# A four-layer convolution network on one core: statistics as a pipeline of loads, group norms split in pieces, earlier pacing of layer 1, and longer runs in layer 2

## The chip, the cores and the metric

The kernel runs on one core of one Trainium2 chip. The metric is the device time of one execution in microseconds (us), and the comparison is made with the median of several executions. Fewer microseconds is better. The core's engines are named as in the profile: PE multiplies matrices (PEld is its load of weights), DVE works on vectors, ACT evaluates functions and copies, POOL is a general vector engine, and SP issues most transfers. Transfers of all queues run on 16 DMA engines.

## The reference

The input x has shape (4, 384, 64, 64). There are four layers, each of the form x = x + layer(gn(x)), where gn is a group norm over 32 groups of 12 channels, without weights:

```python
def _gn(v, G=32, eps=1e-5):
    g = v.reshape(B_, G, C_ // G, H_, W_)
    m = jnp.mean(g, axis=(2, 3, 4), keepdims=True)
    s = jnp.var(g, axis=(2, 3, 4), keepdims=True)
    return ((g - m) / jnp.sqrt(s + eps)).reshape(v.shape)

# layer 0: attention of 4096 positions on the first 96 channels
q, k, v = split(bn(w_qkv @ layer_norm(x[:, :96])))
out = v @ softmax(q^T k / 4)^T
y = bn(w_proj @ relu(concat(out, x[:, 96:])))
# layer 1: w_in, a filter on 8x8 patches by FFT, a 3x3 depthwise convolution
t = dwconv3(irfft2(rfft2(patches(w_in @ x)) * fft_filter))
y = w_out @ (gelu(t[:192]) * t[192:])
# layer 2: depthwise 3x3 and 5x5, each with a norm over batch and image
tok = bn(kw0 * bn(dw3(x)) + kw1 * bn(dw5(x)) + x * c1_w + c1_b)
tok = tok * sigmoid(...);  ch = tok + bn(cm_w2 @ gelu(bn(cm_w1 @ tok)))
y = gate * ch + (1 - gate) * x
# layer 3: a depthwise 7x7 convolution whose kernel is made from mean and maximum of x
```

## The kernel before

**Layers 0 and 1 (phase_a).** The 384 channels lie as three column groups (j = 0, 1, 2) of 128 partitions; an image is 4096 columns, taken in 8 tiles of 512. `attention(b)` works one batch of layer 0 in 64 steps: 8 query tiles by 8 blocks of keys, each step some score matmuls, an exponential on ACT and the `av` matmuls. Beside it `side_by_side` advances a second generator, `others(b)`: the statistics of x for the next batch (`x_norm(b + 1)`), layer 1 of the batch before (`layer1(b - 1)`), and the queries, keys and values of the next batch (`qkv(b + 1)`). Every piece yields its weight, and `per_step` says how much weight is to be done by which attention step. Layer 1 of the last batch runs after the attention, alone. A framework places the instructions on the engines in an order that it works out from the program; within an engine they run in that order.

`x_norm(b)` loads 24 tiles of 128 x 512 (two buffers "xs", for batch 0 nine buffers that the queries take later), and has DVE run bn_stats on each right after its load. `norm_of_stats` aggregates them and `norm_of_groups` turns them into the group norm: a sum over channels on PE (`gn_pg`), a subtraction and squares on DVE, again PE (`gn_pv`), and a reciprocal square root. For batch 0 all this stands ahead of everything else, and `centered`, the first step of `qkv`, then loads the first 96 channels again (`ln_x`). Between the two stands a branch on a bound for the scores; its other side isn't taken here. `layer0_end` leaves statistics from which `norm1` is made when the attention of a batch ends; `layer1` begins with it.

**Layer 2's convolutions (phase_b).** A unit is 32 channels of all four batches; there are 12 units, and each has 16 calls of `conv53`, for two channels each. One call multiplies the image strips `z` with banded Toeplitz matrices (`toep`) that hold both kernel sizes, 3x3 and 5x5; 12 matmuls come from it. `matrices53(n)` builds a matrix by multiplying taps (`w53`, 320 KB for four calls, loaded by `taps53`) with a band mask, on DVE for even n and the first four, on POOL for the rest; it runs two calls ahead, with four buffers. `conv53` copies the result from PSUM into `d_o` (ACT), takes its statistics (bn_stats on DVE), and after every fourth call writes d_o to the scratch tensors `d53`, one for each kernel size, in runs of 4 KB. `conv_norms(u)` ends the unit: it makes scale and shift of both sizes from the statistics (`cn_rep` and `cn_m` on PE, in between ACT and DVE). During the next unit `unit_tok(u)` reads d53 back (`c_d`, 96 reads of 512 KB in all, whose runs are 512 bytes), adds the two sizes and the input (`tok_m`), and stores the sum to `tok`. `unit_strips(u + 1)` loads the next unit's input (`unit_x`, 2048 columns), normalizes it on ACT and transposes it on PE (`strip_m`) into z. Strips and tok take turns, one piece behind each conv53. The loads, the reads of d53 and the stores of tok are issued on SP's queue, the writes of d53 on ACT's.

After the last unit, `tok_stats` waits for the last sums, and the 1x1 convolutions of layer 2 (phase_ef) and layer 3 (phase_g) follow; the change does not touch these.

Of the kernel before, what the change touches and what calls it, by code (L numbers as in the profile page):

```python
# [40 lines left out]
UNITS = C // 32  # L41

# [238 lines left out]
class _Builder:  # L281
    def __init__(self, ctx, tc, ins, out):
# [32 lines left out]
        self.d53 = [  # L315
            [self.dram.tile([32, B, 32, P], F32, tag=f"d{i}{u}", name=f"d_{i}_{u}") for u in range(UNITS)]
            for i in range(2)
        ]
# [110 lines left out]
    def norm_of_groups(self, mv):  # L429
# [7 lines left out]
        nc.vector.tensor_add(d[:, :, 0], d[:, :, 0], mv[:, :, 1])  # L437
        pv = self.of_groups("gn_pv", d)[:, :, 0]
# [69 lines left out]
    def phase_a(self, strips):  # L508
# [3 lines left out]
        with ExitStack() as ctx:  # L512
# [8 lines left out]
            self.probs = attention.enter_context(tc.tile_pool(name="a_probs", bufs=2, side="right"))  # L521
            self.center = self.const(cp, "center", PD)
# [8 lines left out]
            for k in ("r0", "m0", "n0"):  # L531
                setattr(self, k, cp.tile([P, NJ, B], F32, tag=k, name=k))
            self.qkv_weights(cp)
            for _ in self.x_norm(0):
                pass
# [6 lines left out]
            for _ in self.qkv(0, q, k4, vt):  # L542
                pass
# [38 lines left out]
    def others(self, b, nxt):  # L582

        if b + 1 < B:
            yield from self.x_norm(b + 1)
# [7 lines left out]
    def side_by_side(self, b, steps, others):  # L595

        per_step = ((176 if b else 0) + (42 if b + 1 < B else 0)) / 64
# [20 lines left out]
    def norm_of_stats(self, st):  # L618
        mv = self.sm([P, NJ, 2], "gn_mv")
        for j in range(NJ):  # L620
            self.nc.vector.bn_aggr(mv[:, j, :], st[:, j].rearrange("p a b -> p (a b)"))
        return self.norm_of_groups(mv)
# [8 lines left out]
    def x_norm(self, b):  # L631

        st = self.stats_tile("x_st")
        for i in range(8):
            for j in range(NJ):

                x = self.wk("x_in", "xs", 2) if b else self.big.tile([P, 512], F32, tag="q", name="x_in0", bufs=9)
                self.nc.sync.dma_start(x, self.ins["x"][b][:, j, i * 512 : (i + 1) * 512])
                self.nc.vector.bn_stats(st[:, j, i, :], x)
            yield 0.5  # L640
        r, gm, n, _ = self.norm_of_stats(st)
# [3 lines left out]
    def centered(self, b, i):  # L645
# [4 lines left out]
        nc.sync.dma_start(x, self.ins["x"][b][0:PD, 0, i * 512 : (i + 1) * 512])  # L650
        nc.vector.tensor_scalar(
            x, x, self.m0[0:PD, 0, b : b + 1], self.r0[0:PD, 0, b : b + 1], ALU.subtract, ALU.mult
# [27 lines left out]
    def qkv(self, b, q, k4, vt):  # L680
# [3 lines left out]
        xc[0] = self.centered(b, 0)  # L684
        yield 1.0
        xn[0] = self.layer_norm(xc[0])
        xc[1] = self.centered(b, 1)
        yield 2.0
        for i in range(8):
            if i + 2 < 8:  # L690
                xc[i + 2] = self.centered(b, i + 2)
# [1343 lines left out]
```

## Time and profile before

| what | value |
|---|---|
| median of 3 executions | 4879.94 us (4866.37 to 4882.83) |
| the profiled execution, its own time | 4868.55 us |
| span of the profiled execution, first to last instruction | 4866.7 us |
| PE's mean granted clock, full speed being 1 | 0.950 |
| DMA packets in all | 345857, of which 172295 under 2 KB |
| first exponential of the attention | at 75.2 us |
| layers 0 and 1 beside each other end, layer 1 of batch 3 starts | 2161 to 2201 us |
| layer 2: convolutions | 2478 to 3045 us |
| layer 2: first 1x1 convolution | at 3087.8 us |
| layer 3 | 4096 to 4867 us |

The times in the lower rows are counted from the span's first instruction. The profile covers one execution, so its durations add up to that execution's time and not to the median. PE is counted as busy while a matmul is in flight, at whatever clock it was granted: a stretch with a clock of 0.5 can be full and still slow. The costliest groups of instructions in layer 2's convolutions have these lines (line, engine, operation, output and inputs, shapes, count; busy time and mean of one in ns; idle time of the engine before them with what ended most of it):

```profile
L1289 POOL TENSOR_TENSOR toep<-w,band 128x1280 f32<-128x1280 f32 x94 | 272.2, 2900 | 307.0 <-PE conv_m L1308 201.1
L1308 PE MATMUL conv_m<-toep,z 128*128 128x192 f32 (+1 forms) x2304 | 447.0, 356 | 17.8 <-DVE toep L1289 17.6
```

An idle engine costs nothing by itself: POOL is idle for 307.0 us there since its matrices are needed no sooner than PE's convolutions free their buffers.

### The profile page before, as it was taken

The page shows a single profiled execution, that of the slowest core. Times are in us where ns is not written, and L with a number is a line of the kernel's source. Part 1 is how long each engine was busy: PE and PEld are TensorE (multiplying, and loading weights), DVE is VectorE, ACT ScalarE, POOL GpSimd, SP SyncE. Part 2 cuts the span into 40 slices and gives each one's busy share as a digit, 9 for nine tenths or more (in the row PEclk, how much of TensorE's full clock was granted, in tenths as well). Part 3 has the DMA queues.
Part 4 walks back from the last instruction along what each step waited for, and adds up shares of the span by engine and source line. Part 5 has one row for each costly group of instructions (what it writes and reads, how often), then busy time and mean ns, then how long its engine had stood idle before and what let it go on. Part 6 is the DMA issues. An engine that isn't in the chain of part 4 may idle for free. (4 is left out here: it accounts for less than half of the span.)

```text
span 4866.7 us, 49663 instructions
## 1 busy us (share of the span) xinstructions
PE 4413.5 (91%) x18441; PEld 2456.1 (50%) x18441; DVE 2901.2 (60%) x4642; ACT 1998.2 (41%) x2974; POOL 728.9 (15%) x594
## 2 busy tenths in 40 slices
PE   6899999999999999988978889699999997778888
PEld 2233444344443444435468888344444443667888
DVE  6766566655566455566867778555521113667898
ACT  3454344444444443436345556211133334753321
POOL 1000000000000000000034445000000001225544
PEclk8999999999999999999989989899999998788999
DMA  4211212121211111113259999866664444895776
GB/s 159 79 51 48 80 65 72 46 79 33 75 55 67 48 52 52 64 51 124 73 176 296 280 286 308 279 254 253 239 236 151 156 156 160 314 341 185 230 255 232
DMA packets 345857, 749.23 MB, mean 154 GB/s; under 512 B 22684, under 2 KB 172295, under 8 KB 336647
## 3 DMA queue, kind: packets, MB, share of 16 engines
q1 hardware_dynamic: 279864, 471.92, 31.3%
q0 software_dynamic: 32640, 151.28, 7.9%
q10 hardware_dynamic: 33102, 122.77, 6.5%
q8 instruction: 149, 2.44, 0.2%
q14 instruction: 102, 0.83, 0.1%
HBM read 443.62 MB, written 302.25 MB: 153 GB/s over the span
## 5 line engine op out<-in xcount | busy, mean ns | idle before, releaser
L788 ACT ACTIVATE probs<-sc_s 128x1024 f32<-128x1024 f32 x512 | 496.8, 1020 | 690.6 <-PE av L898 588.2
L898 PE MATMUL av<-probs,vt 128*128 128x512 f32 x1536 | 714.9, 602 | 0.0
L1097 DVE SCALAR_TENSOR_TENSOR acc<-band,vecs,acc 128x512 f32<-128x512 f32 x708 | 496.4, 746 | 45.2 <-POOL band L1058 40.0
L1591 PE MATMUL h_m<-f_h,cm_w_t 128*128 128x512 f32 x1152 | 497.4, 595 | 7.4 <-ACT f_h L1579 7.4
L1308 PE MATMUL conv_m<-toep,z 128*128 128x192 f32 (+1 forms) x2304 | 447.0, 356 | 17.8 <-DVE toep L1289 17.6
L898 PEld LDWEIGHTS av<-probs,vt 128*128 128x128 f32 x1536 | 275.6, 191 | 338.1 <-issue 334.4
L1308 PEld LDWEIGHTS conv_m<-toep,z 128*128 128x128 f32 x2304 | 410.9, 198 | 41.0 <-issue 10.1
L1905 PE MATMUL conv_m<-toep,z 128*128 128x128 f32 x3072 | 393.6, 286 | 37.9 <-POOL toep L1892 19.6
L1905 PEld LDWEIGHTS conv_m<-toep,z 128*128 128x128 f32 x3072 | 379.3, 202 | 39.9 <-POOL toep L1892 19.9
L1537 PE MATMUL h_s<-e_tok,cm_w_t 128*128 128x512 f32 x768 | 363.3, 596 | 4.2 <-DVE e_tok L1522 4.2
L1591 PEld LDWEIGHTS h_m<-f_h,cm_w_t 128*128 128x128 f32 x1152 | 219.8, 191 | 285.0 <-issue 273.9
L780 PE MATMUL sc_s<-q,k 32*128 32x512 f32 x2048 | 310.7, 644 | 19.4 <-ACT probs L788 19.1
L1599 DVE BATCH_NORM_STATS2 h_st<-f_h 128x6 f32<-128x512 f32 x96 | 66.4, 693 | 429.9 <-ACT f_h L1598 429.9
L1289 POOL TENSOR_TENSOR toep<-w,band 128x1280 f32<-128x1280 f32 x94 | 272.2, 2900 | 307.0 <-PE conv_m L1308 201.1
L1020 PE MATMUL t_m<-w_in_t,xb 128*128 128x384 f32 x768 | 279.7, 499 | 4.3 <-DVE coef L1037 4.1
L934 PE MATMUL proj_m<-xm,w_proj_t 128*128 128x512 f32 x576 | 271.6, 611 | 4.9 <-DVE xm L873 4.9
L1544 ACT COPY e_h<-h_s 128x1024 f32<-128x1024 f32 x96 | 97.2, 1012 | 400.3 <-PE h_s L1537 400.3
L1546 DVE BATCH_NORM_STATS2 h_st<-e_h 128x6 f32<-128x512 f32 x192 | 123.5, 685 | 203.8 <-ACT e_h L1544 203.8
L1537 PEld LDWEIGHTS h_s<-e_tok,cm_w_t 128*128 128x128 f32 x768 | 146.6, 191 | 188.7 <-issue 183.3
L941 DVE SCALAR_TENSOR_TENSOR x_res<-proj_m,bn_c,x_res 128x512 f32<-128x512 f32 x96 | 71.8, 748 | 241.0 <-PE proj_m L934 240.8
L1020 PEld LDWEIGHTS t_m<-w_in_t,xb 128*128 128x128 f32 x768 | 143.3, 193 | 142.0 <-issue 60.7
L1537 PE MATMUL h_s<-z,cm_w_t 128*128 128x512 f32 x384 | 196.1, 592 | 0.0
(408 smaller groups left out, 6383.4 us busy)
## 6 DMA issues: line engine op xcount, KB each, us to landing
d<-d_o ACTq DMA_DIRECT2D x96, 512.0 KB
c_d<-d SPq DMA_DIRECT2D x96, 512.0 KB
hid<-e_h ACTq DMA_DIRECT2D x16, 3072.0 KB
f_h<-hid SPq DMA_DIRECT2D x16, 3072.0 KB
x_in<-in_x SPq DMA_DIRECT2D x96, 256.0 KB
x_res<-in_x SPq DMA_DIRECT2D x32, 768.0 KB
xa<-x_res POOLq DMA_DIRECT2D x32, 768.0 KB, 3.7
xa_out<-xa SPq DMA_DIRECT2D x32, 768.0 KB
```

What stands on the lines that cost most here:

```text
L780: nc.tensor.matmul(s[:, g], lhsT=k4[32 * g : 32 * g + 32, c], rhs=q[i][32 * g : 32 * g + 32], start=True, stop=True,)
L788: nc.scalar.activation(p[:, h * 1024 : (h + 1) * 1024], s[:, 2 * h : 2 * h + 2].rearrange("p a b -> p (a b)"), AF.Exp, scale=0.25,)
L898: nc.tensor.matmul(av[0], lhsT=vt[:, 4 * c + v, :], rhs=p[:, v * 512 : (v + 1) * 512], start=c == 0 and v == 0, stop=c == 7 and v == 3,)
L934: nc.tensor.matmul(m, lhsT=self.w_proj[:, j, o * P : (o + 1) * P], rhs=xm[:, j], start=j == 0, stop=j == NJ - 1,)
L1020: nc.tensor.matmul(m[:, 0:C], lhsT=xb[:, j], rhs=self.w_in[:, j, :], start=j == 0, stop=j == NJ - 1,)
L1097: nc.vector.scalar_tensor_tensor(out, src(j, k), w, done, ALU.mult, ALU.add)
L1289: eng.tensor_tensor(t, self.w53[:, at : at + 160].rearrange("p (m n) -> p m n", n=8).unsqueeze(2).to_broadcast([P, 20, 8, 8]), band.rearra ...
L1308: nc.tensor.matmul(m[:, c * 256 + to : c * 256 + to + 64 * (k1 - k0)], lhsT=self.z_[:, at : at + P], rhs=t[:, 10 * c + k0 : 10 * c + k1].r ...
L1537: nc.tensor.matmul(s[:, v, :], lhsT=w1[:, j, o * P : (o + 1) * P], rhs=t[j][:, v * 512 : (v + 1) * 512], start=j == 0, stop=j == NJ - 1,)
L1546: nc.vector.bn_stats(st[:, o, 8 * b + 2 * i + v, :], h[:, o, v * 512 : (v + 1) * 512])
L1591: nc.tensor.matmul(m, lhsT=w2[:, o, j * P : (j + 1) * P], rhs=h[:, o, v * 512 : (v + 1) * 512], start=o == 0, stop=o == 5,)
L1905: nc.tensor.matmul(m[:, ch * P : (ch + 1) * P], lhsT=self.z_[:, at : at + P], rhs=t[:, 8 * c + 2 * i : 8 * c + 2 * i + 2].rearrange("p m a ...
```

## The change

**Statistics of x.** `first_tiles` loads the eight tiles of batch 0 that hold channels 0 to 127 and keeps them; `first_norm` makes mean and scale of channels 0 to 95 from them alone, and `qkv(0)` works on the kept tiles in place of loading them again. The other 16 tiles of batch 0 are done by `x_norm(0, ...)` within `others(0)`, ahead of `x_norm(1)`. `x_norm` now asks for two tiles and takes the statistics of the two asked for a piece earlier; a piece has weight 1.2.

**Group norms.** `norm_of_groups` becomes the generator `norm_steps`, which yields between its halves; the moments are made by `moments`. At the end of a batch's attention only the moments are made (`mv1`), and `layer1` does the rest when it starts.

**Pacing.** `per_step` has other weights, and for the last batch it is divided by 57 in place of 64, so that layer 1 of batch 2 is through seven steps before the attention of batch 3 is.

**Layer 2.** One scratch tensor for a unit holds both kernel sizes side by side, so that d_o is written in runs of 8 KB (one transfer, not two) and read back in runs of 1 KB (48 reads, not 96). The sum of `unit_tok` is written over the unit's input in unit_x and stored from there. Strips are asked for two units ahead, in loads of 1024 columns, and normalized half a tile before they are transposed. `conv_norms` of a unit is issued behind the next unit's first conv53. The matrices run three calls ahead (`LEAD`) with five buffers, the taps have three buffers, and their loads are issued on POOL's queue.

```diff
-        self.d53 = [
-            [self.dram.tile([32, B, 32, P], F32, tag=f"d{i}{u}", name=f"d_{i}_{u}") for u in range(UNITS)]
-            for i in range(2)
-        ]
+        self.d53 = [self.dram.tile([32, B, 32, 2, P], F32, tag=f"d{u}", name=f"d_{u}") for u in range(UNITS)]
...
-    def norm_of_groups(self, mv):
+    def norm_steps(self, mv):
...
+        yield 0.3
...
+            for k in ("r0", "m0", "n0"):
+                setattr(self, k, cp.tile([P, NJ, B], F32, tag=k, name=k))
+            self.x0_st = self.stats_tile("x1_st")
+            self.x0 = self.first_tiles(self.x0_st)
...
             self.qkv_weights(cp)
-            for _ in self.x_norm(0):
-                pass
+            self.first_norm(self.x0_st)
...
-            for _ in self.qkv(0, q, k4, vt):
+            for _ in self.qkv(0, q, k4, vt, self.x0):
...
+        if b == 0:
+            yield from self.x_norm(0, self.x0_st, 0.5)
...
-        per_step = ((176 if b else 0) + (42 if b + 1 < B else 0)) / 64
+        per_step = ((177 if b else 5) + (55 if b + 1 < B else 0)) / (64 if b + 1 < B else 57)
...
-    def norm_of_stats(self, st):
-        mv = self.sm([P, NJ, 2], "gn_mv")
+    def moments(self, st, name="gn_mv", bufs=2):
+        mv = self.sm([P, NJ, 2], name, bufs)
         for j in range(NJ):
             self.nc.vector.bn_aggr(mv[:, j, :], st[:, j].rearrange("p a b -> p (a b)"))
-        return self.norm_of_groups(mv)
+        return mv
...
+    def first_tiles(self, st):
+        tiles = []
         for i in range(8):
-            for j in range(NJ):
-                x = self.wk("x_in", "xs", 2) if b else self.big.tile([P, 512], F32, tag="q", name="x_in0", bufs=9)
+            x = self.big.tile([P, 512], F32, tag="q", name="x_in0", bufs=9)
+            self.nc.sync.dma_start(x, self.ins["x"][0][:, 0, i * 512 : (i + 1) * 512])
+            tiles.append(x)
+        for i, x in enumerate(tiles):
+            self.nc.vector.bn_stats(st[:, 0, i, :], x)
+        return tiles
+    def first_norm(self, st):
+        nc = self.nc
+        mv = self.sm([P, 2], "gf_mv")
+        nc.vector.bn_aggr(mv, st[:, 0].rearrange("p a b -> p (a b)"))
+        m = self.pm("gf_m")
+        nc.tensor.matmul(m[:, 0:1], lhsT=self.group, rhs=mv[:, 0:1], start=True, stop=True)
+        mean = self.m0[0:PD, 0, 0:1]
+        nc.vector.tensor_copy(mean, m[0:PD, 0:1])
+        d = self.sm([P, 1], "gf_d")
+        nc.gpsimd.memset(d, 0.0)
+        nc.vector.tensor_sub(d[0:PD], mv[0:PD, 0:1], mean)
+        nc.vector.tensor_mul(d, d, d)
+        nc.vector.tensor_add(d, d, mv[:, 1:2])
+        nc.tensor.matmul(m[:, 1:2], lhsT=self.group, rhs=d, start=True, stop=True)
+        self.rsqrt(self.r0[0:PD, 0, 0:1], m[0:PD, 1:2])
+    def x_norm(self, b, known=None, piece=1.2):
+        st = self.stats_tile("x_st") if known is None else known
+        tiles = [(i, j) for i in range(8) for j in range(0 if known is None else 1, NJ)]
+        coming = []
+        for n in range(0, len(tiles) + 2, 2):
+            there, coming = coming, []
+            for i, j, x in there:
+                self.nc.vector.bn_stats(st[:, j, i, :], x)
+            for i, j in tiles[n : n + 2]:
+                x = self.wk("x_in", "xs", 2)
                 self.nc.sync.dma_start(x, self.ins["x"][b][:, j, i * 512 : (i + 1) * 512])
-                self.nc.vector.bn_stats(st[:, j, i, :], x)
-            yield 0.5
-        r, gm, n, _ = self.norm_of_stats(st)
+                coming.append((i, j, x))
+            yield piece
+        mv = self.moments(st)
+        yield 0.3
+        r, gm, n, _ = yield from self.norm_steps(mv)
...
-    def centered(self, b, i):
+    def centered(self, b, i, src=None):
         nc = self.nc
         x = self.wk("ln_x", "lx", 2)[0:PD]
-        nc.sync.dma_start(x, self.ins["x"][b][0:PD, 0, i * 512 : (i + 1) * 512])
+        if src is None:
+            src = x
+            nc.sync.dma_start(x, self.ins["x"][b][0:PD, 0, i * 512 : (i + 1) * 512])
         nc.vector.tensor_scalar(
-            x, x, self.m0[0:PD, 0, b : b + 1], self.r0[0:PD, 0, b : b + 1], ALU.subtract, ALU.mult
+            x, src[0:PD], self.m0[0:PD, 0, b : b + 1], self.r0[0:PD, 0, b : b + 1], ALU.subtract, ALU.mult
         )
         s = self.pm("ln_s")
         nc.tensor.matmul(s[0:PD], lhsT=self.center, rhs=x, start=True, stop=True)
...
-        self.norm1 = self.norm_of_stats(st)
+        self.mv1 = self.moments(st, "gn_mv1", 1)
...
-        norm, alone = self.norm1, b == B - 1
+        norm, alone = (yield from self.norm_steps(self.mv1)), b == B - 1
...
-            for n in range(4):
+            for n in range(LEAD + 2):
                 self.matrices53(n)
             for q in range(4):
...
+            strips, behind = self.unit_strips(1), None
+            next(strips)
             for u in range(UNITS):
                 st = self.bt_p.tile([P, 2, 16, 6], F32, tag="st", name="st")
-                strips = self.unit_strips(u + 1) if u + 1 < UNITS else iter(())
                 tok = self.unit_tok(u - 1) if u else self.unit_strips(0)
                 nets = iter(()) if u else self.nets(cp)
                 for n in range(16):
                     if u or n > 1:
-                        self.matrices53(16 * u + n + 2)
+                        self.matrices53(16 * u + n + LEAD)
                     self.conv53(u, n, st)
-                    next(strips if n % 2 else tok, None)
+                    if n == 0 and u:
+                        self.conv_norms(u - 1, behind)
+                    if n % 2:
+                        next(strips, None)
+                    elif n or not u:
+                        next(tok, None)
+                    if n == 15 and u:
+                        next(tok, None)
+                    if n == 14 and not u:
+                        for _ in tok:
+                            pass
                     if n % 3 == 2:
                         next(nets, None)
-                self.conv_norms(u, st)
+                    if n == 15 and u + 2 < UNITS:
+                        strips = self.unit_strips(u + 2)
+                        next(strips)
+                behind = st
+            self.conv_norms(UNITS - 1, behind)
...
-        for i in range(2):
+        tiles = self.unit_x[u]
+        def load(i):
             x = self.bx_p.tile([P, 2048], F32, tag="x", name="unit_x")
-            for b in range(B):
-                nc.sync.dma_start(
-                    x[32 * b : 32 * b + 32], self.x1[b][32 * q : 32 * q + 32, j, i * 2048 : (i + 1) * 2048]
-                )
-            self.unit_x[u].append(x)
-            for h in range(4):
-                if h % 2 == 0:
-                    xh = x[:, 512 * h : 512 * h + 1024]
-                    nc.scalar.activation(
-                        xh, xh, AF.Identity, bias=self.norm_u[:, 1, u : u + 1], scale=self.norm_u[:, 0, u : u + 1]
+            for k in range(2):
+                at = i * 2048 + k * 1024
+                for b in range(B):
+                    nc.sync.dma_start(
+                        x[32 * b : 32 * b + 32, k * 1024 : k * 1024 + 1024],
+                        self.x1[b][32 * q : 32 * q + 32, j, at : at + 1024],
                     )
...
+            tiles.append(x)
+        def norm(k):
+            x = tiles[k // 2][:, k % 2 * 1024 : k % 2 * 1024 + 1024]
+            nc.scalar.activation(
+                x, x, AF.Identity, bias=self.norm_u[:, 1, u : u + 1], scale=self.norm_u[:, 0, u : u + 1]
+            )
+        load(0)
+        norm(0)
+        yield
+        for n in range(8):
+            i, h = n // 4, n % 4
+            x = tiles[i]
+            if j:
...
+            if n == 0:
+                load(1)
+            if n % 2 and n < 7:
+                norm(n // 2 + 1)
+            yield
...
-            self.w53_ahead = self.bt_p.tile([P, 8 * 80], F32, tag="w53", name="w53")
+            self.w53_ahead = self.bt_p.tile([P, 8 * 80], F32, tag="w53", name="w53", bufs=3)
             src = self.ins["c53_t"][n // 64][:, n % 64 * 2 : n % 64 * 2 + 8]
-            self.nc.sync.dma_start(self.w53_ahead, src.rearrange("p c m n -> p (c m n)"))
+            self.nc.gpsimd.dma_start(self.w53_ahead, src.rearrange("p c m n -> p (c m n)"))
...
-        t = self.bt_p.tile([P, 20, 8, 8], F32, tag="toep", name="toep53", bufs=4)
+        t = self.bt_p.tile([P, 20, 8, 8], F32, tag="toep", name="toep53", bufs=LEAD + 2)
...
-            self.d_o = self.bt_p.tile([P, 2, 8, P], F32, tag="d_o", name="d_o")
+            self.d_o = self.bt_p.tile([P, 8, 2, P], F32, tag="d_o", name="d_o")
...
-            for v in range(2):
-                nc.scalar.dma_start(
-                    self.d53[v][u][:, :, 2 * n - 6 : 2 * n + 2].rearrange("y b c n -> (y b) (c n)"),
-                    self.d_o[:, v].rearrange("p c n -> p (c n)"),
-                )
+            nc.scalar.dma_start(
+                self.d53[u][:, :, 2 * n - 6 : 2 * n + 2].rearrange("y b c v n -> (y b) (c v n)"),
+                self.d_o.rearrange("p c v n -> p (c v n)"),
+            )
...
-            d5, d3 = (self.bc_p.tile([P, 1024], F32, tag=k, name=f"c_{k}") for k in ("d5", "d3"))
-            for v, d in enumerate((d5, d3)):
-                nc.sync.dma_start(
-                    d.rearrange("p (y n) -> p y n", n=P),
-                    self.d53[v][u][8 * i : 8 * i + 8].rearrange("y b c n -> (b c) y n"),
-                )
+            d = self.bc_p.tile([P, 8, 2, P], F32, tag="d", name="c_d")
+            o = self.unit_x[u][i // 2][:, i % 2 * 1024 : i % 2 * 1024 + 1024]
+            nc.sync.dma_start(
+                d.rearrange("p y v n -> p y (v n)"),
+                self.d53[u][8 * i : 8 * i + 8].rearrange("y b c v n -> (b c) y (v n)"),
+            )
             for h in range(2):
                 part = slice(h * 512, (h + 1) * 512)
                 last = u == UNITS - 1
                 m = self.psum.tile([P, 512], F32, tag="c" if last else "t", name="tok_m", bufs=4 if last else 1)
                 nc.scalar.activation(
-                    m, self.unit_x[u][i // 2][:, i % 2 * 1024 + h * 512 :][:, 0:512], AF.Identity, bias=s0, scale=self.vec("c1_w")[:, u : u + 1]
+                    m, o[:, part], AF.Identity, bias=s0, scale=self.vec("c1_w")[:, u : u + 1]
                 )
-                nc.vector.scalar_tensor_tensor(m, d3[:, part], s[:, 1:2], m, ALU.mult, ALU.add)
+                mv, ov = (t.rearrange("p (y n) -> p y n", n=P) for t in (m, o[:, part]))
+                of = lambda v: d[:, 4 * h : 4 * h + 4, v]
+                nc.vector.scalar_tensor_tensor(mv, of(1), s[:, 1:2], mv, ALU.mult, ALU.add)
                 k = 2 * i + h
                 nc.vector.scalar_tensor_tensor(
-                    d5[:, part], d5[:, part], s[:, 0:1], m, ALU.mult, ALU.add, accum_out=self.total[:, u, k : k + 1]
+                    ov, of(0), s[:, 0:1], mv, ALU.mult, ALU.add, accum_out=self.total[:, u, k : k + 1]
                 )
                 if h == 0:
                     yield
...
-            nc.sync.dma_start(self.tok[u, :, :, sl].rearrange("b c n -> (b c) n"), d5)
+            nc.sync.dma_start(self.tok[u, :, :, sl].rearrange("b c n -> (b c) n"), o)
```

## The prediction, made before the changed kernel ran

> **What bounds the kernel now.** I read the engine table and the slices first, then tables of busy time by stretch (stretch in us from the span's start; its length; then PE, PEld, DVE, ACT and POOL busy with instruction counts; granted clock; DMA share; GB/s), then PE's waits in the stretches where PE is short.
>
> ```profile
> PE 4413.5 (91%) x18441; PEld 2456.1 (50%) x18441; DVE 2901.2 (60%) x4642; ACT 1998.2 (41%) x2974; POOL 728.9 (15%) x594
> ...
> PE   6899999999999999988978889699999997778888
> ...
> PEclk8999999999999999999989989899999998788999
> ...
> 0.00:40.00 40.00, 3.06 (x15) 1.79 (x15) 21.02 (x65) 6.20 (x13) 11.81 (x39) 1.00 0.77 265
> 69.00:99.00 30.00, 30.00 (x59) 11.99 (x59) 15.48 (x28) 12.85 (x19) 1.56 (x3) 0.50 0.30 90
> 2140.00:2165.00 25.00, 18.61 (x41) 6.69 (x39) 23.92 (x33) 10.05 (x11) 2.04 (x5) 0.98 0.26 90
> 2165.00:2210.00 45.00, 32.39 (x59) 13.54 (x60) 20.37 (x52) 11.54 (x26) 1.45 (x2) 0.67 0.28 97
> 2478.00:2700.00 222.00, 195.83 (x1029) 181.89 (x1029) 165.25 (x342) 126.61 (x272) 109.75 (x38) 0.93 0.88 263
> 2700.00:2900.00 200.00, 175.88 (x956) 162.98 (x955) 149.33 (x299) 118.76 (x254) 92.93 (x33) 0.92 0.94 284
> 2900.00:3045.00 145.00, 129.78 (x708) 119.74 (x706) 114.22 (x232) 88.21 (x193) 69.50 (x24) 0.94 0.96 302
> 3045.00:3090.00 45.00, 6.21 (x21) 4.49 (x22) 22.23 (x77) 18.93 (x32) 0.00 (x0) 0.50 0.94 280
> ```
>
> PE is the bound of most of the span. Only where it is short can the change pay: the first 40 us, the end of batch 3's attention (2140 to 2210), layer 2's convolutions (2478 to 3045) and their drain (3045 to 3090). In the convolutions PE is busy 88% and DMA 88 to 96%. PE's waits there (2478 to 3050), as microseconds in total, times, longest:
>
> ```profile
> PE strip_m L1236 <- ACT unit_x L1229: 24.7, 10, 3.0
> PE conv_m L1308 <- DVE toep L1289: 17.6, 7, 4.9
> PE cn_m L1350 <- DVE z L1241: 6.2, 5, 3.8
> PE cn_rep L1341 <- DVE st L1322: 5.9, 4, 1.9
> PE strip_m L1236 <- ACT z L1243: 5.4, 8, 0.9
> PE cn_rep L1341 <- DVE z L1241: 3.5, 3, 1.2
> ```
>
> They are chains through one tile, not a full engine: DVE and ACT have room.
>
> **What the Trainium skill says.** "TensorE: Matmul & The Clock Gate", What's actually happening: the array runs at half rate by default and activity releases it within some 3.4 us. The 0.50 beside the idle drain agrees; the 0.50 of 69 to 99, with PE busy throughout, does not, so I take clocks from the trace. "Perfetto Trace Analysis", DMA Optimizations: transfers under 2 KB carry a significant overhead each. The trace agrees. In 2478 to 3050 (572 us, 9152 engine-us) queue q10 moved 13824 packets of d, 4 KB each, in a 23.3% share: 154 ns each. Queue q1 took 68.6%, 6278 engine-us; some 15,800 of its 111,040 packets are large (about 2430 at 154 ns), which leaves about 40 ns for each of the 95,232 c_d packets of 512 B. "DMA: Bandwidth & Descriptors", SWDGE vs HWDGE vs iDMA: a transfer issued from GpSimd has its descriptors built by software on that engine. The trace of before shows none in this stage. Same page, Issuing engines are not separate DMA queues: all share 16 engines, so moving the taps to POOL adds no bandwidth.
>
> **1. Prologue.** Before, 24 tiles of x stream from 9.1 to 30.2 us, about 1 us each; the norm ends at 34.4, the branch and the reload of x let DVE center the first tile at 41.1. After, 8 tiles are in by about 15 (9.1 + 7 x 0.9); bn_aggr, two one-column matmuls and a square root end near 19 (chain before: 4.2), the branch costs 3.8 as before, and there is no reload (2.9 of that 41.1). DVE starts near 23: minus 18 (15 to 20). PE's order up to the end of qkv(0) is unchanged.
>
> **2. What the prologue leaves.** 16 tiles of batch 0 join the 72 of batches 1 to 3. In DVE's new order 75 of the 88 fall in attention steps 1 to 19 of batch 0; before, 48 fell in steps 1 to 9 and batch 3's 24 near 530. Counted from step 3, 65 tiles meet PE work of about 82 us (16 steps of 3.92, the undisturbed pace, two projections of 8.5, 2 for small matmuls). If DVE's time decides: at 250 to 400 it is busy 102.3 of 150, so 2.67 per step, plus 65 x 0.69 / 17 = 2.64: 5.3 per step, 90 us, 8 lost. If the round trip of two buffers decides: x_norm(2)'s 24 tiles took 43.5 us (121.0 to 164.5), 1.81 each, so 118 us, 36 lost. Before lost 14.2 (121 to 168, PE 32.8 of 47) and 3.2 at 530. So minus 9 to plus 19; I take plus 6, since loads are now asked for a piece ahead. What waits behind a stats instruction on DVE is av_a, and PE's next av behind it (one such wait was 8.7 before). Parts 1 and 2: minus 12, minus 27 to plus 4.
>
> **3. Norms in pieces, layer 1 of batch 2 paced earlier.** Before, the last av of batch 3 ends at 2161.4 and layer 1's first matmul runs at 2200.9: 39.5 us. In it PE waits 9.8 for acc of the last output row, 4.0 and 2.4 for two norm chains. Layer 1 now advances 177/57 = 3.1 units per step, not 2.75, so its rows and one norm are done before: minus 9.8, minus 3.2 (half the chains), minus 2 for the row's own matmuls, 15 in all. The reciprocal, the last projection and its norm stay. The denser steps can put DVE ahead of PE (23.92 of 25 at the end): back up to 5 if out_m waits before av, and I take 5. Minus 10 (minus 16 to minus 2). At the other three batch boundaries a stretch of about 2.5 us without PE becomes pieces: minus 3 (minus 6 to 0).
>
> **4. Layer 2.** Waits in the order of the new program. The normalization of x comes half a unit's step ahead of the transposes, loads two units ahead: the 24.7 goes. conv_norms moves behind the next unit's first convolution, so st and z are old: of 15.6 for cn_rep and cn_m (6.2, 5.9 and 3.5) 2 stay. With matrices three ahead and five buffers toep's 17.6 loses 9.6; the 4.9 at the start remains, with one more 1.47-us matrix ahead. Idle removed: 24.7 + 13.6 + 9.6 = 48. Not all shows, as a PE that waits less meets the next: DVE has 428 busy of 572, POOL 272, and DMA must follow. I take 60%, 29. The clock in the convolutions (0.93) should rise to 0.95 as waits go: 447.0 x (1 - 0.93/0.95) = 9. DMA: c_d's 1-KB packets cost between 40 (counted by packet) and 80 ns (by byte); at 55, 47,600 of them take 2620 engine-us for 3800: 74 us less of DMA time, so DMA falls from some 520 to 446 busy us in 530 and is no bound. If it is 80, it stays at 520 and allows just 10 to 20 of gain. Part 4: minus 38 (minus 15 to minus 62). unit_x now also holds the result until it is stored, so its six buffers serve two units ahead and one behind: SP's queue can wait there with c_d reads behind it, at nothing while DMA keeps up; if not, it ends in the minus 15. The taps' 45 loads of 320 KB go from SP's queue to POOL's, behind the 2.9-us matrix before them: POOL waited 55.0 us for taps before and DVE 1.0, hidden by lead. I cost this at nothing; without that cover it is the slower rival.
>
> **5. Drain.** One c_d read in place of two per quarter, one d write per four convolutions: minus 4 of 45 (0 to minus 8).
>
> **Sum.** -12 -10 -3 -38 -4 = -67 against the profiled execution's 4868.5: 4801.5. The median shown is 11.4 above that execution, so 4813.
>
> **Rivals.** (a) The convolutions keep a bound: DMA by byte, or DVE's Toeplitz and statistics in place of the strips. For it: share 0.88 to 0.96, DVE first among what PE waits for after strips; against: half the packets. Part 4 gives 15, the rest stays: 4836. (b) The x tiles eat what the prologue saved: part 2 at plus 19 and 3 at minus 2: -18 + 19 - 2 - 3 - 38 - 4 = -46, 4834. For it: 1.81 us per tile measured; against: loads a piece ahead. (c) All of it shows: part 4 at -62, the rest at 29: 4789. (d) Slower: taps late. Each of 45 blocks makes POOL, then PE, wait, because the load is issued behind a matrix that waits for PE's convolution, and DMA at 0.9 delivers late (the 13 waits of before were 4.2 us each). At 1.5 us per block, 45 blocks take back 67 and it is even; at 3 us the time is 4813 + 135 = 4948. Against: the third taps buffer and one block, four convolutions (about 12 us), of lead. That the pacing doesn't do what it says is small: layer 1 of batch 2 may end only with the last step, and part 3 is lost: 4823, counted inside the forecast.
>
> **Numbers.** Forecast 0.52, its own range 4792 to 4832; (a) 0.18, (b) 0.11, (c) 0.09, (d) 0.10. Two in ten outside: the low end covers half of (c), the high end (a) and (b) with parts at their poor bounds, so 4770 to 4872. Under 0.3%, 14.6 us, nothing can be told from no change. (a) and (b) reach into that zone at times; of their 0.29, 0.06 goes to it and 0.02 comes from (d) at low prices. Faster 0.84, same 0.08, slower 0.08.
>
> **What would show it.** Right: DVE's first centering near 23; strip_m's wait for unit_x under 5; DMA share in the convolutions below 0.9 with 1-KB packets at about 55 ns; layer 1 of batch 3 starting 25 us after the last av; the stage at about 530 us for 567. Wrong: PE waiting for av_a or ACT in 60 to 200 for over 36 us; conv_m waiting for toep on POOL over 60; the clock still at 0.93 with waits gone.

## The result and the profile after

The changed kernel takes 4845.64 us (median of 8, 4825.65 to 4856.82) against 4875.34 us for the kernel before (median of 8): a ratio of 0.9935, 95% interval 0.9921 to 0.9949. That is 30 us faster, where 67 had been forecast from the median then known. The profiled execution took 4847.67 us, its span is 4845.8.

The same view as before the prediction, busy time by stretch of the changed kernel (stretch, length, then PE, PEld, DVE, ACT and POOL busy, granted clock, DMA share, GB/s):

```profile
0.00:40.00 40.00, 14.54 (x31) 5.74 (x32) 16.80 (x51) 9.48 (x18) 12.35 (x40) 1.00 0.54 174
...
100.00:240.00 140.00, 98.09 (x688) 29.97 (x684) 106.53 (x156) 48.72 (x56) 9.67 (x12) 0.87 0.49 145
...
2500.00:2600.00 100.00, 98.68 (x559) 93.74 (x558) 84.10 (x182) 58.70 (x139) 70.20 (x33) 1.00 0.86 294
2611.00:2642.00 31.00, 6.38 (x28) 4.88 (x26) 14.28 (x30) 18.19 (x27) 1.81 (x2) 0.55 0.91 284
```

PE works earlier in the first 40 us, and then stands idle for 42 us of the stretch from 100 to 240. In the kernel before it stood for 15 us of the same stretch:

```profile
100.00:240.00 140.00, 125.33 (x809) 39.65 (x812) 103.26 (x151) 58.29 (x73) 2.81 (x5) 0.94 0.28 83
```

In layer 2 the first units run with PE full and the clock at 1.00, which none of the stretches shown of before did. Then PE all but stops for 31 us. Its waits over the convolutions (total, times, longest), to be read against the six lines of the prediction:

```profile
PE strip_m L1303 <- ACT unit_x L1289: 44.3, 15, 15.2
PE conv_m L1379 <- DVE z L1308: 9.8, 4, 6.3
PE cn_rep L1411 <- DVE st L1393: 7.0, 4, 2.1
PE cn_rep L1411 <- DVE z L1308: 4.6, 4, 1.2
PE cn_m L1420 <- ACT cn_four L1408: 1.1, 1, 1.1
```

The wait for Toeplitz matrices (17.6) is gone and cn_m's has shrunk (1.6 in all, from 8.1). But the strips wait longer than before (44.3 for 24.7), cn_rep waits 11.6 for 9.6, and convolutions now wait for z. The sum of all of PE's waits there, some 67 us, is no smaller than it was (65). These marks compare the profiled executions (us; the drain is from the last convolution to the first 1x1 convolution):

| mark | before | changed |
|---|---|---|
| first exponential | 75.2 | 53.8 |
| 29th exponential (of 512) | 194.2 | 156.0 |
| first exponential of batch 1 | 480.1 | 475.7 |
| last exponential of batch 3 | 2148.7 | 2155.1 |
| layer 1 of batch 3 starts | 2200.9 | 2185.5 |
| first convolution of layer 2 | 2478.1 | 2464.8 |
| convolutions, then drain | 562.5, 47.2 | 555.9, 55.9 |
| layer 3, from the last 1x1 convolution on | 777.7 | 767.5 |

### The profile page after: what moved, and what is told of

Read it like the earlier page. It is cut to its first block, busy times and chain, and to the rows that moved or that the text cites. A ratio compares the mean times of both kernels' runs of the same rounds, so it can differ in the third digit from the quotient of the medians.

```text
span 4845.8 us, 49741 instructions
## 1 busy us (share of the span) xinstructions
PE 4399.5 (91%) x18445; PEld 2456.5 (51%) x18445; DVE 2893.2 (60%) x4647; ACT 1998.1 (41%) x2976; POOL 761.9 (16%) x643
## 5 line engine op out<-in xcount | busy, mean ns | idle before, releaser
L1379 PE MATMUL conv_m<-toep,z 128*128 128x192 f32 (+1 forms) x2304 | 445.8, 355 | 9.9 <-DVE z L1308 9.8
L841 PE MATMUL av<-probs,vt 128*32 128x512 f32 x1536 | 187.9, 612 | 14.9 <-DVE av_t L870 14.9
```

What stands on the lines that cost most here:

```text
L841: nc.tensor.matmul(av[k][quarter(g)], lhsT=vt[:, 4 * c + v, quarter(s)], rhs=p[:, v * 512 : (v + 1) * 512], start=c == 0 and not before, s ...
L1379: nc.tensor.matmul(m[:, c * 256 + to : c * 256 + to + 64 * (k1 - k0)], lhsT=self.z_[:, at : at + P], rhs=t[:, 10 * c + k0 : 10 * c + k1].r ...
```

## The experiments

**Which half gives it.** Two kernels put the change together by halves: one has the new code outside phase_b and its helpers, the other has only phase_b, unit_strips, taps53, matrices53, conv53, unit_tok and the d53 tensors new.

> The change's parts 1 to 3 (prologue, norms in pieces, pacing) with layer 2's convolutions as before. Theory A (layer 2's part moved its waits and gave nothing): almost the whole gain is here, ratio to before 0.993 to 0.997 (15 to 35 us less), convolutions 560 to 566 us long and the first 1x1 convolution 13 to 17 us earlier than before. Rival B (both halves gave a like share): ratio 0.997 to 0.999.

> Layer 2's convolutions as changed, all else as before. Theory A: ratio 0.998 to 1.002, units 1 to 4 at 35 to 38 us each and the fifth unit at 65 to 85 us, so that the stage from first convolution to first 1x1 convolution stays within 5 us of 610. Rival B: the stage is 10 us shorter or more, ratio below 0.998; the long fifth unit was chance.

Measured: 0.9967 (0.9956 to 0.9978) for the front, 0.9971 (0.9961 to 0.9982) for layer 2. The front's ratio alone would have fitted theory A; that of layer 2 doesn't, so the theory that layer 2's part gave nothing falls. The halves gain about 16 and 14 us and their product, 0.9938, is the whole. Yet the mechanism that it named is there. A unit is 192 matmuls of conv_m, and all 12 x 192 are recorded; by this count units_only's first three units took 36 to 38 us, the fourth 69 and the fifth 48. (The expectations call the long unit the fifth; it is the fourth.) The stage and drain are no shorter in the profile (617.4 us in units_only; 609.7 before and 618.8 in front_only, both with the old code), so where the 14 us sit has to be asked again below.

**The statistics in batch 0.** A load of x is tied to the newest exponential, and for batches 2 and 3 x_norm's pieces alternate with layer 1's:

```diff
                 x = self.wk("x_in", "xs", 2)
+                if hasattr(self, "gate"):
+                    self.nc.vector.tensor_copy(x[0:1, 0:1], self.gate[0:1, 0:1])
...
+            self.gate = p
...
             if piece is None:
+                yield from norm
                 piece = next(qkv, 0.0)
+            elif piece > 1.0:
+                yield next(norm, 0.0)
```

> The changed kernel, with one addition: each load of x_norm waits for the newest exponential (a one-element copy on DVE into the tile to be loaded), and for batches 2 and 3 the pieces of x_norm alternate with layer 1's. The loads can then not all run in batch 0. If the 75 statistics packed into batch 0's first 19 steps cost the roughly 30 us that the exponentials lose between steps 14 and 32: 15 to 30 us faster than the changed kernel (4815 to 4830), PE idle in 100 to 240 us from 42 to under 15. If DVE's load in batch 0 is not the cause: within 6 us of the changed kernel.

Measured: 4831.31 us, just outside the band on the slow side. The ratio, 0.9928 (0.9908 to 0.9947), can't be told from the changed kernel's 0.9935; a comparison on one chip, which can, follows under "Together". PE's idle time fell by half:

```profile
100.00:240.00 140.00, 119.52 (x796) 35.41 (x790) 103.49 (x179) 53.72 (x63) 2.31 (x4) 0.91 0.33 104
```

20 us are idle in place of 42, where under 15 had been expected. The statistics packed into batch 0 cost PE time, as argued, though spreading them takes away only part. Layer 1 of batch 3 starts at 2173.1, 7 to 12 us sooner than in two executions of the changed kernel. How PE came to wait is told by its waits from 40 to 270 us in the changed kernel:

```profile
PE gn_pv L419 <- DVE gn_d L435: 16.7, 2, 11.2
PE av L841 <- DVE av_t L870: 14.1, 2, 13.8
PE sc_s L818 <- ACT probs L826: 11.1, 6, 5.1
```

and by DVE's over the same time:

```profile
DVE x_st L669 <- DMA x_in<-in_x: 34.2, 35, 3.9
```

DVE takes its instructions in the order in which they were placed. It stands 34.2 us at statistics whose tile has not landed (13.2 in the kernel before), and the copies of av and the small operations of the group norms come behind these in its order, with PE behind them. The longest of PE's waits for av shows it:

```profile
189.98 0.69 DVE L669 BATCH_NORM_STATS2 x_st<-x_in 128x6 f32<-128x512 f32 x1 [3.91 <-DMA x_in<-in_x]
191.44 4.20 PE L841 MATMUL av<-probs,vt 128*32 128x512 f32 x24 [13.81 <-DVE av_t L870]
```

The copy of av stands between the two, at 190.70. In these 13.8 us DVE waits 6.2 us for three tiles, and else works on statistics and on sums of exponentials.

**The prologue by itself.** The statistics go back to the old code, all else stays as changed, but for the weights of x_norm in per_step (0 and 43 for 5 and 55). An excerpt; first_tiles and first_norm go, and x_norm takes each statistic right behind its load:

```diff
-            self.first_norm(self.x0_st)
+            for _ in self.x_norm(0):
+                pass
...
-            for _ in self.qkv(0, q, k4, vt, self.x0):
+            for _ in self.qkv(0, q, k4, vt):
...
-        if b == 0:
-            yield from self.x_norm(0, self.x0_st, 0.5)
```

> The changed kernel with the statistics of x as before (24 tiles ahead, x loaded again for the queries, x_norm with a statistic right behind each load), norms in pieces, pacing and layer 2 as changed. If prologue and first batch together are worth about 12 us, as forecast: 8 to 16 us slower than the changed kernel. If the first batch gives all of it back: within 5 us of it.

> The changed kernel itself, beside the three others on one chip, so that differences of a few microseconds can be read against it. Ratio to before 0.992 to 0.995. Its profile repeats the stages: a fifth unit of 65 to 80 us and a drain of 55 to 57 if these are of the kernel and not of one execution.

Measured on one chip: old_prologue 4837.37 us (0.9928, 0.9909 to 0.9947), the changed kernel 4843.01 (0.9940, 0.9923 to 0.9956). The new prologue gives nothing that can be measured. The exponentials show the gain and its loss: the new prologue leads by 19.9 us at the first (51.6 for 71.5), 35.2 at the 29th (152.8 for 188.0), 14.3 at the 37th, 3.8 at the 65th, 2.0 at the end of batch 0 and none when layer 1 of batch 3 starts (2179.9, 2179.8). The stretch from 105 to 260 us holds the loss, here old_prologue

```profile
105.00:260.00 155.00, 135.20 (x934) 41.73 (x932) 123.34 (x173) 64.81 (x78) 9.58 (x12) 0.94 0.39 116
```

and here the changed kernel:

```profile
105.00:260.00 155.00, 114.54 (x776) 34.55 (x772) 114.34 (x170) 56.28 (x68) 8.65 (x12) 0.88 0.43 130
```

PE is 20.7 us less busy, at a lower clock. The second execution also repeats the long fourth unit (69.1 us, after 69.7) and a drain of 54.4 us, a little under the band written for it. These belong to the kernel.

**The pacing.**

```diff
-        per_step = ((177 if b else 5) + (55 if b + 1 < B else 0)) / (64 if b + 1 < B else 57)
+        per_step = ((177 if b else 5) + (55 if b + 1 < B else 0)) / 64
```

> The changed kernel with the last batch paced over all 64 steps again. If ending layer 1 of batch 2 early is what shortened the tail: last matmul av to layer 1 of batch 3 back from 22 to between 30 and 40 us, the kernel 6 to 16 us slower than the changed one. If the norms in pieces did it: tail within 4 us of 22, the kernel unchanged.

Measured: 4838.58 us, 0.9922 (0.9895 to 0.9950): not slower. By the expectation's own measure, from the last av matmul, the tail is 24.3 us for 22, within the band for norms in pieces. From the last exponential to layer 1 of batch 3 it takes 39.0 us, the changed kernel 29.6 (changed_again) and the old code 52.3 (units_only). So norms in pieces shorten this tail by 13 us and the pacing by 9 more; but with the pacing the last exponential comes 15 us later (2150.3 for 2135.1). The pacing moved work and did not hide it. The end of the attention with 64 steps:

```profile
2169.24 0.39 PE L419 MATMUL gn_pv<-gn_d,group 128*128 128x3 f32 x2 [2.91 <-DVE gn_d L435]
2169.48 0.36 PE L419 MATMUL gn_pg<-gn_mv,group 128*128 128x3 f32 x2
2171.67 0.56 PE L419 MATMUL gn_pv<-gn_d,group 128*128 128x3 f32 x2 [1.82 <-DVE gn_d L435]
```

Both norm chains still run there, ahead of layer 1 at 2174.1, but interleaved: the second gn_pg follows the first gn_pv at once, and the output row, whose sum PE awaited for 9.84 us in the old order, lies ahead of this stretch.

**What limits layer 2.** First the bytes that are in no chain. The kernel leaves out 45 of the 48 loads of taps, so the convolutions use wrong taps:

```diff
-        if n < 16 * UNITS:
+        if n < 12:
...
+        else:
+            self.w53_ahead = self.w53_all[n // 4 % 3]
```

> The changed kernel without 45 of the 48 loads of taps (three are loaded and used over and over, so the convolutions use wrong taps): 14.4 MB less of some 159 MB in the stage, and nothing else moves, since the taps are not in the chain write d, read c_d, sum, store tok, load unit_x. If the stage is bound by the bytes on the 16 DMA engines: 35 to 50 us less in the stage. If it is bound by that chain and its six buffers: less than 12 us.

Measured: 4829.04 us (0.9934, 0.9911 to 0.9957); the stage with its drain took 597.3 us, against 611.8 and 608.0 in the two executions of the changed kernel, so 11 to 15 less. Neither band was met cleanly; it lies nearer the chain's. Nor is it far outside the scatter: in six executions with this stage as changed (the two, units_only, gated_stats, old_prologue, pace64) it took 600.6 to 617.4 us, and the whole kernel's ratio is the changed kernel's. Then the chain's own reads, halved, so that the sums take wrong rows:

```diff
-                d.rearrange("p y v n -> p y (v n)"),
-                self.d53[u][8 * i : 8 * i + 8].rearrange("y b c v n -> (b c) y (v n)"),
+                d[:, 0:4].rearrange("p y v n -> p y (v n)"),
+                self.d53[u][8 * i : 8 * i + 4].rearrange("y b c v n -> (b c) y (v n)"),
...
-                of = lambda v: d[:, 4 * h : 4 * h + 4, v]
+                of = lambda v: d[:, 0:4, v]
```

> The changed kernel with half of each c_d read (four of eight rows, used for both halves, so the sums take wrong rows): 25 MB less in the stage and shorter reads, the same chain otherwise. If bytes decide, by the slope of taps_once (14.4 MB gave 14 us): stage 580 to 592 us. If the wait for the reads in the chain decides: stage 555 to 575, the fifth unit under 50. If neither does (six buffers, stores): stage over 600.

Measured: 4800.55 us (0.9854, 0.9832 to 0.9875) and a stage of 572.7 us, 35 to 39 less for 25 MB. Of all edits to this stage it is the only one that moved it clearly, and the kernel beside the changed one on the same chip is 42 us faster. The time fits the chain's band, but the long unit, which was to be under 50, took 64.0 (69.7 and 69.1 in the changed kernel). What went are the strips' waits after it. In half_read all of them, this line's and 3.1 us for a load itself, lie in the fourth unit:

```profile
PE strip_m L1303 <- ACT unit_x L1289: 16.0, 3, 8.1
```

In the changed kernel the strips wait 24.6 us in the fourth unit and 19.7 later, in the kernel before 19.9 after the fourth. The units side by side (us; the columns add up to the convolutions and their drain):

| kernel | units 1 to 3 | unit 4 | units 5 to 12 | drain |
|---|---|---|---|---|
| before | 135.5 | 50.8 | 376.2 | 47.2 |
| changed | 110.6 | 69.7 | 375.7 | 55.8 |
| changed_again | 111.2 | 69.1 | 373.2 | 54.4 |
| half_read | 111.4 | 64.0 | 349.0 | 48.2 |

Units 5 to 12 of before, changed and half_read:

```profile
2664.40:3040.50 376.10, 337.59 (x1839) 313.34 (x1838) 289.04 (x581) 224.62 (x484) 179.50 (x62) 0.93 0.95 291
2645.10:3020.70 375.60, 338.29 (x1837) 315.66 (x1838) 281.78 (x573) 221.10 (x480) 196.20 (x90) 0.92 0.85 282
2629.20:2978.10 348.90, 329.48 (x1837) 309.30 (x1838) 276.94 (x565) 216.96 (x475) 196.15 (x90) 0.95 0.76 256
```

The change took the DMA share from 0.95 to 0.85 there and no time: PE is idle for 37 us as before (38). Half the reads took 18 us of idle time and 9 of PE's busy time away, at a higher clock (0.95 for 0.92).

Per MB half_read gives 1.4 to 1.6 us, and the taps 0.7 to 1.0 if their few microseconds are real. So the bytes that the sums wait for count more. It excludes neither the engines' load nor the latency of the reads, as both were halved.

**The number of loads, and the drain.** The first reads of d53 came 64 us after the first convolution (47 before), behind 48 loads of unit_x on SP's queue (16 before), of which the last 29 took until 2529. The queue of the changed kernel (start, duration of the group):

```profile
2463.95 65.23 SPq L1281 DMA_DIRECT2D unit_x<-x  x29
2529.22 2.84 SPq L1445 DMA_DIRECT2D c_d<-d  x3
...
2619.03 0.34 SPq L1472 DMA_DIRECT2D tok<-unit_x  x1
2619.47 0.43 SPq L1445 DMA_DIRECT2D c_d<-d  x1
2626.29 4.35 SPq L1281 DMA_DIRECT2D unit_x<-x  x8
```

In the first stretch the loads waited for writes of d (SP's waits from 2450 to 2529):

```profile
SPq L1281 <- DMA d<-d_o: 50.5, 6, 21.1
```

A load of unit_x needs nothing of d. But in this trace the transfers that SP and ACT issue report their landing on the same eight semaphores, taken in turn, and a load waits on its own until the older transfer there has landed. The longest wait, 21.1 us, ends at 2485.4 on a semaphore whose last user is the write of d issued at 2479.3: SP stood until the convolutions had filled that d_o and the write had landed. So SP's queue could not run ahead of ACT's, and the reads behind the loads came late. What this costs was not tested.

Two kernels try the number of loads, by loads of 2048 columns, and the old place of the last unit's norms, with a piece of the sums behind every convolution of that unit:

```diff
-            for k in range(2):
-                at = i * 2048 + k * 1024
-                for b in range(B):
-                    nc.sync.dma_start(
-                        x[32 * b : 32 * b + 32, k * 1024 : k * 1024 + 1024],
-                        self.x1[b][32 * q : 32 * q + 32, j, at : at + 1024],
-                    )
+            for b in range(B):
+                nc.sync.dma_start(
+                    x[32 * b : 32 * b + 32], self.x1[b][32 * q : 32 * q + 32, j, i * 2048 : (i + 1) * 2048]
+                )
```

> The changed kernel with unit_x loaded 2048 columns at a time (8 transfers of 256 KB for a unit, as before the change, not 16 of 128 KB). SP's queue stood 50 us in units 0 and 1 at these loads, waiting for older transfers to end (d writes above all), with the c_d reads behind them. If that number of transfers delays the reads, and so the sums, the stores and the loads of the fifth unit: first c_d read 10 to 25 us sooner after the first convolution, the fifth unit at 45 to 60 us in place of 74, and the kernel 8 to 25 us faster than the changed one. If the stage is limited by what the DMA engines carry or by the six buffers: within 6 us of it, the fifth unit still over 65.

```diff
+                    last = u == UNITS - 1
+                    if n == 0 and last:
+                        self.conv_norms(u - 1, behind)
                     self.conv53(u, n, st)
-                    if n == 0 and u:
+                    if n == 0 and u and not last:
                         self.conv_norms(u - 1, behind)
                     if n % 2:
                         next(strips, None)
-                    elif n or not u:
+                        if last:
+                            next(tok, None)
+                    elif n or not u or last:
                         next(tok, None)
```

> The changed kernel, but in the last unit alone conv_norms stands ahead of the unit's first convolution, as before the change, and the sums advance at every step. If the later start of the sums is what lengthened the drain from 47 to 56 us (last convolution to first 1x1 convolution): drain 46 to 51, the convolutions at most 3 us longer, 3 to 8 us faster in all. If the transfers of the last quarters take the time: drain 54 to 58.

Measured: wide_loads 4839.40 us, 0.9935 (0.9911 to 0.9959), the ratio of the changed kernel. Its first read comes 58 us after the first convolution, its fourth unit takes 68.3. The number of loads is not the cause. That the reads stand behind these loads in SP's queue at all was not changed in any run, and stays an untested rival, as do the shared semaphores. In the three kernels with wide loads the drain is 49 to 51 us, in the others with the new layer 2 and whole reads 54 to 58; but the stage is no shorter (607 us on average, 609 in the six named above).

last_unit_norms 4836.76 us, 0.9933 (0.9912 to 0.9954), with a drain of 55.4: the place of the norms isn't what lengthened it. In the changed kernel's drain DVE waits 12.3 us for the c_d reads (4.16 and 4.97 us are the longest). half_read shortens that wait to 3.7 and the drain to 48.2, so the reads bear on it. But the wide loads shorten it too, with whole reads, and in the kernel before DVE waited 9.5 us for reads in a drain of 47.2. What lengthened the drain is not settled.

**Together.**

> Both additions at once: the gated statistics of x and the loads of 2048 columns. If the two losses are separate, the gains add: the 14 us of gated_stats (4831 for 4845) plus what wide_loads gives, 4805 to 4825. If they share one cause, no faster than the better of the two.

> Gated statistics, loads of 2048 columns, and 64 steps for the last batch. The pacing moved work and gave nothing, so: within 6 us of gated_wide, 12 to 25 us faster than the changed kernel (ratio to before 0.989 to 0.992).

Measured: 4824.56 us, 0.9906 (0.9881 to 0.9930), and 4829.18 us, 0.9915 (0.9896 to 0.9934). gated_wide ran beside wide_loads (4839.40), from which only the gating and its alternating pieces part it, and is 15 us faster; only one of six executions of wide_loads is below the slowest two of gated_wide. gated_wide_64 is 14 us faster than the changed kernel beside it (4843.01), and starts layer 1 of batch 3 at 2164.6. That the wide loads add to the gated statistics can't be told from these intervals.

## Why the prediction was right in sign and twice too large

The 4845.64 us lie above the forecast's own range (4792 to 4832), and inside the wide one only because that was stretched for the rivals. Both that lie near came in part. As rival (a) had it, layer 2's part gave about 15 us, though not by its mechanism: DMA did not stay at its old time, and the strips are still first among PE's waits. As rival (b) had it, the tiles of x ate what the prologue saved.

**Prologue (forecast minus 18): right.** DVE centers the first tile at 25.9 us (23 forecast). The first exponential is 17.7 us sooner than in units_only and 19.9 sooner than in old_prologue. The 38 us of the first table at the 29th are partly chance: units_only runs the same front as before and is 9.9 us ahead of it there.

**What the prologue leaves (plus 6 taken, minus 9 to plus 19 shown): mis-sized.** The two parts were to give 12 and gave nothing, with old_prologue even 5.6 us lower in the median. The upper bound, the round trip of two buffers at 1.81 us for each tile, was right in size: the lead of 19.9 us at the first exponential is gone at layer 1 of batch 3. The reason for taking the middle, "since loads are now asked for a piece ahead", failed: the piece ahead exists in the program's text, but DVE's order has the statistics packed so that their distance in time is gone (34.2 us of waits).

**Norms in pieces and pacing (minus 13 with the other boundaries): right in sum, wrong in part.** front_only gained 16 and the prologue nothing, so by subtraction the norms carry it (they were not tried alone), above all with 13 us in the tail. The pacing was credited with the hidden output row (9.8 and 2); it moved that row, and the denser steps took back all of it, not 5, though pace64's interval is wide.

**Layer 2 (minus 38) and drain (minus 4): the step that failed.** 14 us came. Part 4 took 48 us of idle time away and let 29 show; in the profiles PE is idle for 64 us of the convolutions, where it was for 62. Only some of the named waits went: the matrices' 17.6 to nothing, cn_m's 8.1 to 1.6. cn_rep's was to go with them and rose from 9.6 to 11.6, and the strips' wait, which was to be under 5, is 44.3. The clock was to rise from 0.93 to 0.95 for 9 us and is 0.91; conv_m takes 445.8 us for 447.0.

That DMA "falls from some 520 to 446 busy us in 530" came near: the queues' shares in 2464 to 3036 (51.4, 22.9, 8.5, 0.3 and 0.1% of 572 us) make 476. What failed is the term beside it, SP's wait "at nothing while DMA keeps up". The share in the convolutions fell from 0.92 to 0.83, and the wait came all the same, because unit_x now holds the sums until they are stored. The first three units carry no transposes and ran at 36 to 38 us in place of 40 to 48. Their sums fell behind: the last store of a unit's sums was issued 72, 79 and 89 us after the next unit had begun, where before it was at most 59. The fourth unit carries the transposes for the fifth (u = 4 in the program), whose second buffer is free only when the sums of the second unit (u = 1) are stored (the last at 2619; loads resume at 2626). PE then stands:

```profile
2621.02 1.97 PE L1303 MATMUL strip_m<-ident,unit_x 128*128 128x128 f32 x8 [3.98 <-ACT unit_x L1289]
2638.16 1.97 PE L1303 MATMUL strip_m<-ident,unit_x 128*128 128x128 f32 x8 [15.17 <-ACT unit_x L1289]
```

Of the 25 us that the first three units saved the fourth gave back 19, and the other eight took what they had taken. The chain of the buffers is read from the queue and these lines, and it repeats in every kernel with the new layer 2. What sets its length is not settled: half the reads took only 5.5 us off the fourth unit's waits (19.1 for 24.6), and did more in the units after it and in the drain. The rest may lie in the late first read, to which SP's waits for writes of d led; more buffers, reads ahead of the loads, or semaphores for the reads alone were not tried.

**Packets.** 1-KB packets were taken at 55 ns. From after to half_read, queue q1 went from a 51.4% share of 572 us (60636 packets) to 42.3% of 530 us (38082): 1117 us of one engine's time for 22554 packets, so an estimate of 50 ns each, against the 40 ns estimated for 512 bytes. The Trainium skill, "Perfetto Trace Analysis", DMA Optimizations, says that transfers under 2 KB carry a significant overhead each. These estimates agree: half as many packets cost five eighths as much.

**Drain.** It lengthened by 9 us where 4 less was forecast: one read of 1 MB in the place of two of 512 KB left DVE waiting 12.3 us for reads, where it had waited 9.5. That is 3 us of the 9; the rest stays open. **The slower rival (d), late taps,** did not happen: PE waited for no POOL matrix.

**What stays open.** Of the 14 us of layer 2's part the profiles place about 5 in the stage (614 us on average over two executions with the old code, 609 over six with the new) and 6 in layer 3, which the change does not touch. Single executions scatter as much as that, so the place of these few microseconds is not settled.

## What to carry to other kernels

A wait that is removed pays only as far as the next supply. Before crediting it, follow one unit's data through read, sum and store in the new order, and look for the first place where a buffer must come back; units that reach this place sooner wait there, even if the mean share of the DMA engines falls. Where a scheduler places instructions, a distance in the program's text is no distance in time: here loads that depended on nothing were pulled forward as one block, and a small dependency on recent work spread them out again. A shorter tail is no gain by itself: read the mark ahead of it as well, as work may have been moved in front of it.

## What the runs showed of the hardware that was not expected

Layer 3 has the same instruction order on every engine in all these kernels, and took 767.3 to 778.7 us from the last 1x1 convolution to the end. Before and units_only share their first instructions, yet in the stretch from 40 to 105 us the granted clock was 0.76 in one and 0.92 in the other:

```profile
40.00:105.00 65.00, 56.97 (x124) 21.75 (x124) 38.76 (x70) 23.96 (x38) 2.60 (x5) 0.76 0.36 106
```

That is before. The next is units_only, with 58 more matmuls in the same time:

```profile
40.00:105.00 65.00, 59.31 (x182) 22.71 (x183) 49.00 (x92) 29.59 (x46) 4.17 (x8) 0.92 0.41 126
```
